# The next chunk's norm ahead of the gates in the plan of a state-space layer's second slot

## The chip, the cores and the metric

The kernel runs on one core of a Trainium2 chip. The metric is the device time of one execution in microseconds, the median over runs. The kernel before has 25287.4 us (3 runs, 25274.87 to 25290.24).

## The reference

Four layers on x of shape (8, 192, 56, 56) in float32, each `x = x + layer(group_norm(x))`: an involution (layer 0) and three selective state-space layers. The change touches layer 1, which is cut here to what matters:

```python
xn = layer_norm(tokens(group_norm(x)))           # over the 192 channels, L = 3136 tokens an image
xs = three slices of 64 channels, each a sequence of its own (3 * 8 sequences)
xi, z = split(xs @ in_proj_W.T)                  # 512 + 512
xc = silu(depthwise_conv4(xi));  dt, B, C = parts of xc @ x_proj_W.T, dt through softplus
h[t] = h[t-1] * exp(dt * A) + dt * xc * B[t]     # 512 x 16 states
y = (sum over states of h * C + xc * D) * silu(z)
out = proj(layer_norm(y @ out_proj_W.T + skip * xs))
```

## The kernel before, in words

The tokens of an image are cut into 7 chunks of T = 448, so there are 56 chunks. A chunk of layer 1 is three jobs, one for each slice of 64 channels; the code calls the slice a slot (0, 1, 2). A job is 16 units: 4 blocks `j` of 128 inner channels by 4 quarters `q` of the 16 states. A chunk has 48 units; the text numbers them 0 to 47, 16 to 31 being slot 1's.

A unit k does on each engine, in the order of the loop in `ssm_layer`:

- DVE: two scans (`scan`, L758), one for each half of its rows, and for even units the input product `inputs_by_vector` (L754) of unit k+1; in the last unit of a block (`q == 3`) the gate product `gated` (L792).
- POOL: for odd units the input product `inputs_by_pool` (L748) two units ahead, then `readout` (L767), the product with C, of unit k-2. So POOL's queue reads: inputs 35, readout 31, readout 32, inputs 37, and so on.
- ACT: the decays (`da`, L729) of the next unit, the start values (L737), and `keep` (L762), which stores the last state once both scans are done and which the readout waits for.
- PE: `reduce` of unit k-3 (L776, with L773 ahead of it at the first unit of a block, which waits for `gated`), the B row for `inputs_by_vector` (`spread_b`, L723) two units ahead, and filler matmuls (`nothing`, L782).
- SP issues the DMAs, in the order of the program: the loads of a block's operands (`load_ops`, `rep<-ops`, L713, four DMAs), which wait for their buffer; rows of B for POOL's inputs and of C for its readouts (`row_in`, `rows<-bc`, L629). B's rows for the next job's units 1 and 3 are issued in units 13 and 15 of a job, C's four rows in a job's first four units.

Beside the scan of one job the next job is prepared: convolution, projections, softplus, gates. These steps are spread over the 32 half units of a job by `places`, each step with a cost, over stretches that `bounds` sets. For slot 1's job, which prepares slot 2, the last stretch has half units 22 to 31, and it holds the gate steps of slot 2 and, in this job alone, the layer norm of the next chunk: `gates` (L1039) adds `norm()` (L972) of the next chunk where `i == 2`. The plan of a half unit is run (`bg.run`) ahead of the half unit's scan. A step's `rest`, such as an eviction, is called when a later step asks for it by its number `left`.

`norm()` is: normalize (L330, ACT, in place in `xg`), an average over channels (PE, L537), subtract (DVE, L543) and square (ACT, L545), the second average (L537), Ln and Exp (ACT, L549, L550), scale (DVE, L554), affine (ACT, L559), and `slices`: two small copies on ACT (L986, L987), or two memsets on POOL (L982, L983) for an image's first chunk, and eight DMAs from SP into `xs` (L991). `xs` has two buffers. The first convolution of the next chunk's slot 0 (L1026) reads it, and that one is prepared in slot 2's job, from its first half unit on. A gate step is one matmul (L1044) and its eviction to `zs` (ACT, L674). PE's short outputs share two PSUM banks (`mm_tile`).

The costs that `places` spreads are given with the steps, and a pause is a step that does nothing:

```python
return [
    Step(lambda: average(t), center, 0, nk), flushed(), pause(1.5),
    Step(lambda: average(lambda: st["sq"]), rstd, 0, nk), flushed(), pause(),
    Step(None, scale, 0), pause(1.5), Step(None, affine, 0), pause(),
]
```

Of the kernel before, what the change touches and what calls it, by code (L numbers as in the profile page):

```python
# [49 lines left out]
def pause(cost=1.0):  # L50
    return Step(None, lambda: None, 9, cost)
# [35 lines left out]
def conv_mamba_stack(ctx: ExitStack, tc: tile.TileContext, a, out):  # L87
# [16 lines left out]
    def mm_tile():  # L104
        return banks.mm.tile([128, 512], F32, tag="mm", name="mm")
# [424 lines left out]
    def layer_norm_steps(pool, t, p, nk, gam, bet):  # L530

        st = {}

        def average(src):
            st["ps"] = mm_tile()
            for i in range(nk):
                nc.tensor.matmul(  # L537
                    st["ps"][:p, :T], lhsT=lavg[:p, :p], rhs=src()[:, i, :], start=(i == 0), stop=(i == nk - 1)
                )

        def center():
            v, pm = t(), st["ps"]
            nc.vector.tensor_sub(v, v, pm[:p, :T].unsqueeze(1).to_broadcast([p, nk, T]))  # L543
            st["sq"] = pool.tile([CP, 3, T], F32, tag="sq", name="sq")[:p, :nk, :]
            nc.scalar.activation(st["sq"], v, AF.Square)  # L545

        def rstd():
            pv = st["ps"]
            nc.scalar.activation(pv[:p, :T], pv[:p, :T], AF.Ln, bias=eps[:p, :])  # L549
            nc.scalar.activation(pv[:p, :T], pv[:p, :T], AF.Exp, scale=-0.5)  # L550

        def scale():
            v, pv = t(), st["ps"]
            nc.vector.tensor_mul(v, v, pv[:p, :T].unsqueeze(1).to_broadcast([p, nk, T]))  # L554

        def affine():
            v = t()
            for i in range(nk):
                nc.scalar.activation(v[:, i, :], v[:, i, :], AF.Identity, bias=bet[:, i : i + 1], scale=gam[:, i : i + 1])  # L559
# [6 lines that stand above are left out]
# [105 lines left out]
    def evict(w, dst, src, m):  # L671

        if w.inb is None:
            nc.scalar.copy(dst, src)  # L674
        else:
            nc.scalar.activation(dst, src, AF.Identity, bias=w.inb[:, m : m + 1])  # L676

    def gate_steps(pool, w, u, z_mm, z_cost):

        zps = {}  # L680

        def gate(j):
            zps[j] = z_mm(j)

        def gate_out(j):
            if j == 0:
                u.zs = pool.tile([128, w.nd, T], F32, tag="zs", name="zs", bufs=2)
            evict(w, u.zs[:, j, :], zps[j][:, :T], w.nd + j)

        return [Step(lambda j=j: gate(j), lambda j=j: gate_out(j), 1, z_cost) for j in range(w.nd)] + [pause(0.5)]  # L690
# [274 lines left out]
    def mamba_jobs(pool, w):  # L965
        jobs = []
        chunks = Chunks(pool, 1)
        cks = chunks.all
        for ck in cks:
            c = ck.c  # L970

            def norm(c=c, ck=ck):  # L972
                def gnorm():
                    ck.xn = chunks.normalized(ck, None, 1)

                def slices():

                    xn = ck.xn
                    xs = pool.tile([128, 3, T + 3], F32, tag="xs", name="xs", bufs=2)
                    ck.xs = xs  # L980
                    if c == 0:
                        nc.gpsimd.memset(xs[:64, :, 0:2], 0.0)  # L982
                        nc.gpsimd.memset(xs[64:, :, 0:3], 0.0)  # L983
                    else:
                        before = cks[ck.place - 1].xs
                        nc.scalar.copy(xs[:64, :, 0:2], before[:64, :, T : T + 2])  # L986
                        nc.scalar.copy(xs[64:, :, 0:3], before[64:, :, T : T + 3])  # L987
                    for h in range(2):
                        for p0, p1, i, src in ((0, 64, 0, xn[0:64, 0, :]), (0, 32, 1, xn[64:96, 0, :]),
                                               (32, 64, 1, xn[0:32, 1, :]), (0, 64, 2, xn[32:96, 1, :])):  # L990
                            nc.sync.dma_start(out=xs[64 * h + p0 : 64 * h + p1, i, 2 + h : T + 2 + h], in_=src)  # L991

                return (
                    [Step(None, gnorm, 2)] + layer_norm_steps(pool, lambda: ck.xn, CP, NCT, g96, b96)
                    + [Step(None, slices, 2)]
                )

            ck.norm = norm

            def finish(c=c, ck=ck):  # L1000
                pps = {}

                def proj(t):
                    pps[t] = mm_tile()
                    for i in range(3):
                        nc.tensor.matmul(
                            pps[t][:CP, :T], lhsT=w.projw[:, i, t * CP : (t + 1) * CP], rhs=ck.y[:, i, :],
                            start=(i == 0), stop=(i == 2),
                        )

                def add(t):
                    nc.vector.scalar_tensor_tensor(
                        ck.x[:, t, :], pps[t][:CP, :T], w.projb[:, t : t + 1], ck.x[:, t, :], ALU.add, ALU.add
                    )

                return layer_norm_steps(pool, lambda: ck.y, 64, 3, g64, b64) + [
                    Step(lambda t=t: proj(t), lambda t=t: add(t), 1, 3) for t in range(NCT)
                ] + [pause()] + chunks.leave_steps(ck)

            for i in range(3):  # L1020

                def prepare(u, *beside, i=i, ck=ck, norm=norm):
                    def conv_mm(j):
                        pm = mm_tile()
                        for k in range(2):
                            nc.tensor.matmul(  # L1026
                                pm[:, :T], lhsT=w.inconv[:, k, j * 128 : (j + 1) * 128],
                                rhs=ck.xs[:, i, 2 - 2 * k : 2 - 2 * k + T], start=(k == 0), stop=(k == 1),
                            )
                        return pm  # L1030

                    convs, *others, stores = project_steps(pool, w, u, conv_mm, 2, *beside)
                    if i == 0:
                        stores = stores + [Step(None, lambda: chunks.fetch_next(ck), 2)]
                        if ck.place == 0:
                            convs = norm() + convs
                    return convs, *others, stores

                def gates(u, i=i, ck=ck):  # L1039
                    after_gates = cks[ck.place + 1].norm() if i == 2 and ck.place + 1 < len(cks) else []  # L1040

                    def z_mm(j):
                        pm = mm_tile()
                        nc.tensor.matmul(  # L1044
                            pm[:, :T], lhsT=w.inz[:, j * 128 : (j + 1) * 128], rhs=ck.xs[:64, i, 2 : T + 2], start=True, stop=True
                        )
                        return pm

                    return gate_steps(pool, w, u, z_mm, 1) + after_gates

                def after(u, i=i, ck=ck, finish=finish):
                    def out_proj():
                        u.ps = mm_tile()
                        nc.tensor.matmul(u.ps[:64, :T], lhsT=skip_d, rhs=ck.xs[:64, i, 2 : T + 2], start=True, stop=False)
                        for j in range(4):
                            nc.tensor.matmul(u.ps[:64, :T], lhsT=w.outw[:, j, :], rhs=u.zs[:, j, :], start=False, stop=(j == 3))

                    def leave():
                        if i == 0:
                            ck.y = pool.tile([64, 3, T], F32, tag="y", name="y")  # L1060
                        nc.scalar.copy(ck.y[:, i, :], u.ps[:64, :T])

                    def fetch():
                        if i == 2:
                            chunks.fetch_again(ck)

                    return fetch, [Step(out_proj, leave, 1, 5)], finish() if i == 2 else []

                jobs.append((i, c == 0, prepare, gates, after))
        return jobs  # L1070

# [74 lines left out]
    with ExitStack() as stack:  # L1146
        banks.y = stack.enter_context(tc.tile_pool(name="ps_iy", bufs=1, space=PSUM))
        banks.mm = stack.enter_context(tc.tile_pool(name="ps_im", bufs=6, space=PSUM))
        pool = stack.enter_context(tc.tile_pool(name="inv", bufs=1))
        with tc.manual_schedule():  # L1150
            involution(pool)
    for layer, w in enumerate((w1, w2, w3), 1):
        with ExitStack() as stack:
            scan_banks(stack)
            pool = stack.enter_context(tc.tile_pool(name=f"ssm{layer}", bufs=1))
# [75 lines left out]
```

## Time and profile before

| | |
|---|---|
| median of 3 runs | 25287.4 us |
| the profiled execution | 25314.83 us |
| its span | 25313.0 us |
| PE, mean granted clock | 83% busy, 0.827 |
| DVE | 89% busy, 22641.3 us |
| ACT | 67% busy, 16946.5 us |
| POOL | 92% busy, 23383.1 us |
| scans L758 (8064) | 15928.1 us, 2011 ns each |
| readouts L767 (4032) | 14746.3 us, 3675 ns each |
| inputs on POOL L748 (2016) | 8038.2 us, 3987 ns each |

Busy shares are means over the whole span, in which layer 1 is about 1630 to 17380 us. An idle time is put down to what ended it: `A <- B` means that A stood until B was done. In a timeline the columns are start and length in us, engine (SPq is SP's issue of DMAs), line, operation, output and inputs, a count of merged instructions, and in brackets the idle time ahead with what ended it. A DMA's length there is its issue, not its transfer.

### The profile page before, as it was taken

To read this page: it belongs to the slowest core of one execution; us is meant where nothing else is said; L and a number is where in the kernel's file an instruction comes from. 1 tells how busy PE (TensorE), PEld (TensorE's weight loads), DVE (VectorE), ACT (ScalarE), POOL (GpSimd) and SP (SyncE) were. 2 spreads that over 40 slices of the span, in tenths; PEclk is the share of its full clock that TensorE was granted. 3 is DMA by queue.
4 is the path that set the end of the run, shared out by engine and by line. 5 is a ranking of instruction groups with operands and counts; after the bars stand their busy time and mean duration, and the time that the engine had idled before them with its cause. 6 is when DMAs were issued, how large, how long until landed. Compare 5 with 4: busy or idle time off the path is not lost.

```text
span 25313.0 us, 232064 instructions
## 1 busy us (share of the span) xinstructions
PE 21123.4 (83%) x71870; PEld 6720.0 (27%) x71870; DVE 22641.3 (89%) x15661; ACT 16946.5 (67%) x32354; POOL 23383.1 (92%) x6772
## 2 busy tenths in 40 slices
PE   9988888888888888888888888888888887888888
PEld 3322222222222222222222222222333332333332
DVE  8879988998899889998998899897999998999998
ACT  1137776767766776766776676676777776777776
POOL 4469999999999999999999999998999998999999
PEclk9988777877777777777777787778888888888888
DMA  4433333333333333333333333333444443444443
GB/s 106 105 101 123 122 119 117 122 121 119 118 122 121 119 120 119 123 119 119 123 119 120 121 120 118 121 119 108 139 141 136 139 140 120 141 138 139 138 145 128
DMA packets 1184872, 3132.61 MB, mean 124 GB/s; under 512 B 163756, under 2 KB 446404, under 8 KB 1183496
## 3 DMA queue, kind: packets, MB, share of 16 engines
q1 hardware_dynamic: 1180824, 3116.70, 37.9%
q8 instruction: 564, 9.24, 0.1%
q14 instruction: 684, 5.60, 0.1%
q10 hardware_dynamic: 2800, 1.06, 0.0%
HBM read 2399.92 MB, written 555.55 MB: 117 GB/s over the span
## 4 chain that ended last, share of the span: by engine, by line
DVE 29%; PE 25%; ACT 19%; issue 11%; POOL 9%; DMA 6%; SPq 2%; DVEq 0%; POOLq 0%; ACTq 0%
DVE uhg L758 20%; ACT da L729 8%; DVE uhg L754 6%; POOL uhg L767 6%; PE y L776 4%; PE mm L635 4%; POOL uhg L748 3%; PE mm L416 3%; DMA rows<-bc 3%; PE y L782 2%; ACT L569 2%; PE y_inv L451 2%; PE y L773 2%; PE mm L612 2%; DMA rep<-ops 2%
## 5 line engine op out<-in xcount | busy, mean ns | idle before, releaser
L758 DVE TENSOR_TENSOR_SCAN uhg<-da,uhg 128x898 f32<-128x898 f32 x8064 | 15928.1, 2011 | 1284.0 <-ACT da L729 1261.9
L767 POOL TENSOR_TENSOR uhg<-uhg,rows 128x1792 f32<-128x1792 f32 x4032 | 14746.3, 3675 | 654.5 <-ACT carry L762 425.9
L729 ACT ACTIVATE da<-rep,k 128x448 f32<-128x448 f32 x16128 | 10255.9, 636 | 1816.6 <-DVE uhg L758 1438.7
L748 POOL TENSOR_TENSOR uhg<-rep,rows 128x1792 f32<-128x1792 f32 x2016 | 8038.2, 3987 | 375.5 <-DMA rep<-ops 206.2
L776 PE MATMUL y<-uhg,k 128*32 128x448 f32 x32256 | 4756.8, 666 | 562.0 <-POOL uhg L767 560.2
L754 DVE TENSOR_TENSOR uhg<-rep,b 128x1792 f32<-128x1792 f32 x2016 | 4031.8, 2000 | 658.9 <-PE b L723 615.1
L762 ACT COPY carry<-uhg 128x4 f32<-128x4 f32 x4032 | 787.3, 195 | 3514.0 <-DVE uhg L758 3464.3
L773 PE MATMUL y<-xc,w_d 128*128 128x448 f32 x2016 | 1522.0, 850 | 1580.5 <-DVE zs L792 1580.3
L782 PE MATMUL y<-w_d,k 128*128 128x448 f32 (+1 forms) x5166 | 2465.1, 586 | 0.0
L1026 PE MATMUL mm<-xs,k 128*128 128x448 f32 x2688 | 1289.7, 617 | 479.6 <-DMA xs<-xg 318.7
L776 PEld LDWEIGHTS y<-uhg,k 128*32 128x32 f32 x32256 | 695.1, 117 | 3664.1 <-issue 2204.0
L1082 PE MATMUL mm<-v,w_in 96*128 96x448 f32 x2688 | 1427.9, 662 | 199.7 <-ACT zs L676 92.4
L635 PE MATMUL mm<-dbl,w_dt 36*128 36x448 f32 (+1 forms) x2016 | 1469.0, 840 | 127.0 <-ACT k L617 127.0
L782 PEld LDWEIGHTS y<-w_d,k 128*128 128x128 f32 x5166 | 1035.4, 215 | 1486.5 <-issue 1459.8
L436 POOL TENSOR_TENSOR x<-x,one 96x448 f32<-96x448 f32 x560 | 633.3, 1135 | 668.3 <-DVE one L428 650.7
L612 PE MATMUL mm<-dbl,k 16*16 16x448 f32 x1120 | 692.7, 707 | 515.7 <-ACT dbl L605 515.7
L428 DVE TENSOR_TENSOR prod<-mm,shifted 128x448 f32<-128x448 f32 x1680 | 932.6, 609 | 207.8 <-PE mm L416 187.3
L1109 PE MATMUL mm<-xin,w_conv 128*128 128x448 f32 x2688 | 1076.4, 543 | 2.0 <-ACT xin L674 1.0
L773 PEld LDWEIGHTS y<-xc,w_d 128*128 128x128 f32 x2016 | 455.0, 265 | 2191.9 <-DVE zs L792 1509.5
L647 PE MATMUL mm<-xc,k 128*128 128x448 f32 x2016 | 983.7, 599 | 31.1 <-DVE dt L650 30.3
L723 PE MATMUL b<-k,k 96*128 96x448 bf16 x2016 | 819.1, 406 | 129.9 <-DVE uhg L754 129.8
L593 ACT ACTIVATE xc<-mm,k 128x448 f32<-128x448 f32 x1008 | 615.3, 627 | 438.9 <-PE mm L1026 327.1
(134 smaller groups left out, 19720.0 us busy)
## 6 DMA issues: line engine op xcount, KB each, us to landing
rep<-ops SPq DMA_DIRECT2D x4032, 448.0 KB, 5.7
ops<-dt SPq DMA_DIRECT2D x1008, 448.0 KB, 3.3
rows<-bc SPq DMA_DIRECT2D x1792, 224.0 KB, 6.2
shifted<-xpad SPq DMA_DIRECT2D x672, 179.0 KB, 4.6
xg<-stream SPq DMA_DIRECT2D x168, 336.0 KB, 3.7
xr<-stream SPq DMA_DIRECT2D x168, 336.0 KB, 5.3
stream<-xr SPq DMA_DIRECT2D x112, 336.0 KB, 3.2
xs<-xg SPq DMA_DIRECT2D x224, 112.0 KB, 6.1
```

Source lines behind the costliest of these rows:

```text
L612: nc.tensor.matmul(u.left[m][:NS, :T], lhsT=ident[:NS, :NS], rhs=u.dbl[:NS, :], start=True, stop=False)
L635: nc.tensor.matmul(u.dps[j][:, :T], lhsT=w.dtw[:, j * 128 : (j + 1) * 128], rhs=u.dbl[:nk, :], start=True, stop=True)
L729: nc.scalar.activation(t[:, 64 + 449 * r : 512 + 449 * r], reps[k // NQ][:, 2 * h + r, 0, :], AF.Exp, scale=w.neg_a[:, j * NR + 2 * h + r, ...
L748: nc.gpsimd.tensor_mul(uhg[k][:, :, 1:], reps[k // NQ][:, :, 1, :], b)
L754: nc.vector.tensor_mul(uhg[k][:, :, 1:], reps[k // NQ][:, :, 1, :], b)
L758: nc.vector.tensor_tensor_scan(v, banks.da[h][:, 63:961], v, 0.0, ALU.mult, ALU.add)
L767: nc.gpsimd.tensor_mul(v, v, us[i].rows[1, q].unsqueeze(1).to_broadcast([128, NR, T]))
L773: nc.tensor.matmul(ys[k // NQ][:, :T], lhsT=w.dd[:, j, :], rhs=us[i].xc[:, j, :], start=True, stop=False)
L776: nc.tensor.matmul(y[32 * r : 32 * r + 32, :T], lhsT=fold, rhs=uhg[k][:, r, 1:], start=False, stop=(q == NQ - 1))
L782: nc.tensor.matmul(ys[k // NQ][:, : nd * 112], lhsT=zeros, rhs=w.dd.rearrange("p j e -> p (j e)")[:, : nd * 112], start=False, stop=False,)
L1026: nc.tensor.matmul(pm[:, :T], lhsT=w.inconv[:, k, j * 128 : (j + 1) * 128], rhs=ck.xs[:, i, 2 - 2 * k : 2 - 2 * k + T], start=(k == 0), st ...
L1082: nc.tensor.matmul(pm[:, :T], lhsT=w.inw[:, k, m * 128 : (m + 1) * 128], rhs=ck.v[:, k, :], start=(k == 0), stop=(k == NCT - 1),)
```

## The change

In the list of steps that `gates` returns, the next chunk's norm comes first and the four gate steps after it. The list's costs, and the stretch over which they are spread, stay the same. It concerns the 55 jobs that scan slot 1 of a chunk with a chunk behind it.

```diff
                 def gates(u, i=i, ck=ck):
-                    after_gates = cks[ck.place + 1].norm() if i == 2 and ck.place + 1 < len(cks) else []
+                    normed = cks[ck.place + 1].norm() if i == 2 and ck.place + 1 < len(cks) else []
...
-                    return gate_steps(pool, w, u, z_mm, 1) + after_gates
+                    return normed + gate_steps(pool, w, u, z_mm, 1)
```

## The prediction

> **What bounds the kernel now.** I read the page first (busy times, costliest groups), then the waits of layer 1 alone, then the timeline of one chunk boundary engine by engine. The edit touches layer 1 only (1632 to 17380 us of the span), so one row of the busy times by stretch sets the scene; its columns are PE, PEld, DVE, ACT, POOL, granted clock, DMA share and GB/s:
>
> ```profile
> 1632.00:17380.00 15748.00, 12801.13 (x40062) 3735.45 (x40060) 14149.18 (x8559) 10986.03 (x20990) 15077.12 (x4046) 0.79 0.36 120
> ```
>
> POOL is busy 15077 of 15748 us. It is idle for 671 us in the whole layer, and no reordering that leaves POOL its work can win more. DVE has 1599 us idle. These are the longest waits there:
>
> ```profile
> DVE uhg L758 <- ACT da L729: 715.2, 415, 3.8
> DVE uhg L754 <- PE b L723: 572.0, 276, 5.8
> ...
> POOL uhg L767 <- ACT carry L762: 378.1, 365, 4.0
> POOL uhg L767 <- DMA rows<-bc: 224.6, 56, 5.1
> ...
> PE mm L1026 <- DMA xs<-xg: 318.7, 56, 8.1
> ```
>
> POOL waits 56 times, once a chunk, about 4 us, for a row of C (`rows<-bc`), and PE waits 56 times, once a chunk, 5.7 us, for `xs`. Both DMAs leave by SP. One boundary (slot 1 of chunk 25 ends, slot 2 begins), SP, then PE, DVE and POOL:
>
> ```profile
> 8839.82 1.31 SPq L629 DMA_DIRECT2D rows<-bc  x2
> 8861.25 2.97 SPq L713 DMA_DIRECT2D rep<-ops  x4
> 8864.37 7.96 SPq L991 DMA_DIRECT2D xs<-xg  x8
> 8872.44 2.52 SPq L629 DMA_DIRECT2D rows<-bc  x4
> ...
> 8872.95 3.32 PE L1026 MATMUL mm<-xs,k 128*128 128x448 f32 x4 [5.72 <-DMA xs<-xg]
> ...
> 8876.68 2.02 DVE L754 TENSOR_TENSOR uhg<-rep,b 128x1792 f32<-128x1792 f32 x1 [4.89 <-PE b L723]
> ...
> 8860.05 3.67 POOL L767 TENSOR_TENSOR uhg<-uhg,rows 128x1792 f32<-128x1792 f32 x1 [1.46 <-ACT carry L762]
> 8863.68 3.98 POOL L748 TENSOR_TENSOR uhg<-rep,rows 128x1792 f32<-128x1792 f32 x1
> 8867.63 3.65 POOL L767 TENSOR_TENSOR uhg<-uhg,rows 128x1792 f32<-128x1792 f32 x1
> 8875.61 3.67 POOL L767 TENSOR_TENSOR uhg<-uhg,rows 128x1792 f32<-128x1792 f32 x1 [4.33 <-DMA rows<-bc]
> ```
>
> The norm is the last thing in slot 1's plan, so its eight `xs` copies leave in the last unit, behind four `rep` loads. They take 7.96 us to issue: the last two stand until those loads land (releases at 8869.58 and 8871.81). Behind them on SP stand the four rows of slot 2; the first leaves at 8872.44, lands at 8875.48, and POOL idles 4.33 us. PE stands 5.72 us at slot 2's first convolution, the B row (L723) queued behind it is late, and DVE idles 4.89 us. Both of the busiest engines lose their time to one late step, so the loss is on the path. The copies start at 8584.45, 8864.37 and 9144.19 in three chunks running: 279.9 us a chunk.
>
> **The change, by parts.** Each of 55 chunks (the last has no next) moves one norm: on ACT normalize 2 x 0.70, square 0.95, Ln and Exp 0.58 + 0.52, affine 2 x 0.70; on PE two averages of 1.74 and 1.67; on DVE subtract 1.08 and scale 1.08; on SP eight copies; on ACT two small copies (0.19 + 0.20), which for an image's first chunk are two memsets on POOL (0.10 each). Four gate matmuls (3.51 together) and four evictions (about 0.5 each) go the other way. Nothing is removed; the filler matmuls of the stretch go from 5 to 6 (0.46 us, on PE, hidden while PE waits). In half units counted 22 to 31 from the plan's costs:
> before: gates 22, 22, 23, 23; normalize and average 24; subtract 26; second average 27; Ln, Exp 28; scale 29; affine and copies 31.
> after: normalize and average 22; subtract 23; second average 24; Ln, Exp 26; scale 27; affine 28; copies and two gates 29; gates 30 and 31.
>
> I place the moved steps on the shown chunk; unit numbers count 48 a chunk, so slot 1 is 16 to 31.
>
> *DVE.* PE ends the folds of unit 24 at 8839.76, where the gates start now; the average starts there instead and ends 8841.5. DVE is free at 8840.17, so subtract waits 1.43 us (it waits 1.31 now, two units later). The second scan of unit 27 starts at 8842.6 for 8840.08, and by unit 29 the moved 1.08 us and its wait are given back: 8848.4 for 8848.26. Scale follows in unit 29 at 8852.3 without its present wait of 0.68, as Ln and Exp now end a unit ahead of it. Unit 31 scans at 8859.7 for 8860.17: 0.45 us gained.
>
> *SP.* The affine starts on ACT when the decays of unit 30 end (8856.9), its first half ends near 8857.6, and the first copy leaves at 8857.7 for 8864.37. No rep load is ahead of it: the previous DMAs landed by 8846.7 (6.3 us after 8840.47). Copies that wait for nothing leave every 0.62 us (8866.21, 8866.85, 8867.49), so eight take 5.0, to 8862.7. The fifth, the last that slot 2's first convolution needs, leaves at 8860.2 and lands by 8866 at the median under load (6.1): the convolution, due about 8867, does not wait.
>
> *What the copies are moved past.* Here the change adds a wait. Now the second row of the pair at 8839.82, B's row for unit 35, leaves 24 us early. In the new order it stands behind the copies, and SP stands still for the affine: it leaves at 8862.7 for 8840.47. Behind it come the four rep loads (8863.4 to 8865.9, for 8861.25) and then C's row for unit 32 (8866.0, for 8872.44). How fast a row lands has two rows: 3.0 to 3.1 us behind `xs` copies (the three of 8872.44 to 8873.76), 6.3 right behind rep loads (8839.82). B's row is the first kind: 8865.7. C's row is the second: 8872.3.
> The Trainium skill, page "DMA: Bandwidth & Descriptors", section "Anatomy of one DMA — SWDGE (gpsimd) path", fits a transfer as about 2.0 us plus its bytes over 436 GB/s, for GpSimd's queue; an estimate from it for a 224 KB row is 2.5 us, below the 3.0 measured here for SP's, and with it POOL's chain below would gain another 0.5 us a chunk. The measured row is used.
>
> *POOL.* Readout 27 waits for the later scan (8844.9 for 8843.70); readout 30 starts at 8860.4 for 8860.05, so the 1.46 us gap moves forward and shrinks to a few tenths. POOL is free for inputs 35 at 8864.05, its row lands at 8865.7 and is seen at 8865.9: a new stall of 1.85. Then inputs (3.98) and readout 31 (3.65) put readout 32 at 8873.5 for 8875.61; its row landed at 8872.3. POOL gains 2.1 us there.
>
> *DVE at unit 33.* The convolution's bank is free when ACT has evicted the third gate, 8867.6; at half clock (3.32 for 4 records, as 8872.95 shows) it and the B row end near 8871.5, at full clock near 8870. DVE wants the row at 8871.3. So 4.89 of wait become 0 to 0.6, and with the 0.45 DVE gains 4.7 to 5.3.
>
> *Which of the two counts.* In layer 1 POOL holds DVE 7 times, 6.6 us in all (`DVE uhg L758 <- POOL uhg L767` among DVE's waits), while DVE's scans, through ACT's carry, hold POOL 365 times. So DVE runs ahead and POOL catches up in its own gaps. Averaged over chunks 7 to 54, the gaps ahead of readouts 42, 8, 12 and 14 of the units that follow are 0.85, 0.31, 0.75 and 1.19: 3.1 us that a later POOL fills, and another 1.57 at readouts 15 and 26. 2.1 + 3.1 = 5.2: POOL can follow. I take 4.9 us a chunk, 55 x 4.9 = 270 us. The profiled execution took 25314.8 us (span 25313.0 and 1.8 around it); 25314.8 - 270 = 25045. It is 27.4 above the median 25287.4, from which I subtract the same: 25017, said as 25020.
>
> **Rivals.**
> *PE's clock.* Rows of PE busy by stretch (columns as above):
>
> ```profile
> 8867.30:8870.70 3.40, 0.00 (x0) 0.00 (x0) 3.40 (x3) 2.39 (x7) 3.40 (x2) 1.00 0.99 280
> 8870.70:8877.60 6.90, 4.65 (x7) 2.33 (x8) 2.01 (x2) 1.87 (x4) 2.57 (x2) 0.51 0.53 178
> 8898.00:8901.50 3.50, 0.07 (x1) 0.08 (x2) 3.50 (x3) 2.92 (x7) 3.50 (x2) 0.99 0.00 0
> 8901.50:8921.90 20.40, 20.40 (x44) 4.94 (x45) 17.84 (x10) 14.45 (x30) 20.40 (x7) 0.50 0.28 94
> ```
>
> After an empty 3.4 us the clock halves. The second time it stays halved for 20.4 us though PE is busy throughout, and DVE waits for PE in unit 41 (1.4 us a chunk on average). PE's idle stretch before it is about 5.3 us, so a shift of 5 us against a window of 3.413 us (the spacing of the clock's records) can make it miss a whole empty window; then 1.4 more is won, and the chunk falls to near 80 windows, 273.1 (now 82: 279.9). Gain 6.3 to 6.8 a chunk, 347 to 374 us: 24913 to 24940. Against it: it can also halve elsewhere, and 81 windows (276.5, gain 3.4) is as near.
> The Trainium skill, page "TensorE: Matmul & The Clock Gate", section "Part 1: The HAM clock gate", says an idle window of about 3.4 us throttles PE and one busy window releases it, the window running free. The first half agrees with the rows above; the second does not (20.4 busy us at 0.50). By the rule PE would be at full clock from about 8905 and that wait would not be there to win.
> *POOL holds the gain.* If the catching up fails, only POOL's 2.1 us come, or 3.4 if the clock locks the chunk at 81 windows: 116 to 187 us, 25100 to 25172. For it: POOL's 96%. Against: who holds whom, above.
> *The wait only changes its place.* With the copies as slow as now (8.0) and B's row at the median of its line (6.2), it lands at 8871.9, 6.2 later than I put it. POOL's 2.1 become a loss of 4.1, of which its gaps take back 3.1 to 4.7: 55 lost to 33 won, 25254 to 25342, mostly no change that can be told.
> *Slower: SP held by the copies.* The same row decides. With copies at 8.0 and the row at the longest of its line (9.9), it lands at 8875.6: the stall is 9.9 longer than I put it, POOL at readout 32 is 7.8 behind today, its gaps give 4.7 back, and 3.1 x 55 = 170 us are lost: 25457. It decides from a landing past 8872.5. For it: a row that used to leave 24 us early now sits behind a wait for ACT. Against: the rep loads that slow the copies now come after them.
> That page on DMA says in the same section that any semaphore wait happens on the issuing sequencer ahead of dispatch, which is this rival's mechanism; the wait of SP from 8852.27 to 8861.21 agrees.
>
> **How the numbers follow.** Forecast (4 to 6 a chunk, 24960 to 25070) 0.47; clock 0.15; POOL holds 0.18; same place 0.10; slower 0.10. What a measurement of this kernel can tell from no change is about 0.2%, 50 us. Faster 0.80, same 0.10, slower 0.10. The range takes in the clock rival with a little more and POOL's rival with its 2.1: 24900 to 25210.
>
> **What would show it.** Right: the `xs` copies ahead of the rep loads on SP, about 5 us in all; `PE mm L1026 <- DMA xs<-xg` and `POOL uhg L767 <- DMA rows<-bc` gone; `DVE uhg L754 <- PE b` down by some 250 us; `POOL uhg L748 <- DMA rows<-bc` new, under 2 us each, 55 times; copies 275 us apart. Wrong: that new wait at 5 us or more, PE's half clock spreading in units 32 to 41, or chunks still 279.9 apart.

## The result, and the profile after

The changed kernel takes 25021.5 us (4 runs, 25018.75 to 25031.88) against 25281.1 (4 runs): ratio 0.9897, 95% interval 0.9885 to 0.9909. Its profiled execution took 25031.9 us, 282.9 below that of before; the forecast took 270 off.

The same boundary as before (slot 1 of chunk 25 into slot 2), in the timeline of the changed kernel: SP, then PE, DVE and POOL.

```profile
8724.55 4.98 SPq L991 DMA_DIRECT2D xs<-xg  x8
8729.57 0.59 SPq L629 DMA_DIRECT2D rows<-bc  x1
8730.28 2.49 SPq L713 DMA_DIRECT2D rep<-ops  x4
8732.86 8.05 SPq L629 DMA_DIRECT2D rows<-bc  x4
...
8734.49 1.77 PE L1026 MATMUL mm<-xs,k 128*128 128x448 f32 x4 [0.21 <-ACT zs L674]
...
8708.73 1.08 DVE L543 TENSOR_TENSOR xg<-xg,mm 96x896 f32<-96x896 f32 x1 [1.49 <-PE mm L537]
...
8738.17 1.98 DVE L754 TENSOR_TENSOR uhg<-rep,b 128x1792 f32<-128x1792 f32 x1
...
8732.75 3.99 POOL L748 TENSOR_TENSOR uhg<-rep,rows 128x1792 f32<-128x1792 f32 x1 [1.98 <-DMA rows<-bc]
8736.70 7.30 POOL L767 TENSOR_TENSOR uhg<-uhg,rows 128x1792 f32<-128x1792 f32 x2
```

The copies leave ahead of the rep loads and take 4.98 us for 7.96. The convolution waits 0.21 us, and not for `xs`; DVE's product of unit 33 (8738.17) has no wait ahead of it; POOL's readout 32 (the second of 8736.70) has none. In their place POOL waits 1.98 us for the B row, which now leaves behind the copies. The waits of layer 1 (to 17120 us), DVE's then POOL's; columns are total, times and longest:

```profile
DVE uhg L758 <- ACT da L729: 731.9, 407, 3.8
DVE uhg L754 <- PE b L723: 341.1, 221, 2.7
...
POOL uhg L767 <- ACT carry L762: 199.7, 171, 4.0
POOL uhg L748 <- DMA rows<-bc: 83.2, 42, 3.0
...
POOL uhg L748 <- PE y L782: 25.0, 13, 2.0
```

DVE's wait for the B row falls by 231 us (572.0 before), POOL's waits for DVE through the carry by 178, and POOL's wait for C's row (224.6) is gone. In its place stands the new one for B's row ahead of inputs 35, 2.0 us a chunk: the 83 us of its line, and the 25 that the view puts down to PE.

### The profile page after: what moved, and what is told of

It is laid out like the page before. It is cut to its first block, busy times and chain, and to the rows that moved or that the text cites. A ratio compares the mean times of both kernels' runs of the same rounds, so it can differ in the third digit from the quotient of the medians.

```text
span 25030.1 us, 232222 instructions
## 1 busy us (share of the span) xinstructions
PE 21294.5 (85%) x71980; PEld 6723.5 (27%) x71980; DVE 22624.9 (90%) x15661; ACT 16939.4 (68%) x32354; POOL 23378.2 (93%) x6772
## 4 chain that ended last, share of the span: by engine, by line
DVE 33%; PE 27%; ACT 17%; issue 11%; POOL 6%; DMA 5%; SPq 1%; DVEq 0%; POOLq 0%; ACTq 0%
DVE uhg L758 24%; ACT da L729 8%; DVE uhg L754 6%; PE y L776 4%; PE mm L635 4%; POOL uhg L767 4%; PE mm L416 3%; DMA rows<-bc 2%; PE y L782 2%; POOL uhg L748 2%; ACT L569 2%; PE y L773 2%; DMA rep<-ops 2%; PE y_inv L451 2%; PE mm L612 2%
## 5 line engine op out<-in xcount | busy, mean ns | idle before, releaser
L1026 PE MATMUL mm<-xs,k 128*128 128x448 f32 x2688 | 1211.5, 585 | 120.6 <-ACT zs L674 108.7
L1044 PE MATMUL mm<-xs,k 64*128 64x448 f32 x1344 | 860.6, 749 | 98.3 <-ACT zs L674 98.3
```

The source lines that it names most:

```text
L1026: nc.tensor.matmul(pm[:, :T], lhsT=w.inconv[:, k, j * 128 : (j + 1) * 128], rhs=ck.xs[:, i, 2 - 2 * k : 2 - 2 * k + T], start=(k == 0), st ...
```

## The experiments

Theory S is the prediction's: the order of the DMAs on SP, with DVE setting the chunk. G says that the gates' new place and PE matter, P that POOL's time counts us for us, D that DVE's alone does, C that PE's clock takes gains back. The table, to which the verdicts refer, has means over chunks 7 to 54 of each profile: us from one chunk's first scan to the next, DVE's idle time, and the parts of it at subtract and scale (units 27 to 30) and at the B rows of units 33 and 41, and POOL's idle time. The kernel before was measured again with each set of runs, at 25281 to 25309 us; a ratio is to the runs of its own set.

| kernel | median us | chunk | DVE idle | 27-30 | 33 | 41 | POOL idle |
|---|---|---|---|---|---|---|---|
| before | 25281 | 280.6 | 27.7 | 2.7 | 5.0 | 1.4 | 11.3 |
| changed | 25022 | 275.0 | 22.4 | 1.7 | 0.3 | 1.7 | 5.8 |
| e1 copies last | 25202 | 278.5 | 25.8 | 1.7 | 5.0 | 0.6 | 9.3 |
| e2 B row first | 25068 | 275.4 | 22.8 | 1.8 | 0.5 | 1.2 | 6.1 |
| e3 C row first | 25291 | 280.2 | 27.3 | 2.8 | 4.9 | 1.1 | 10.8 |
| e4 rows, copies, reps | 25035 | 275.3 | 22.3 | 3.0 | under 0.2 | 0.9 | 6.2 |
| e5 B row late | 25229 | 278.6 | 25.3 | 2.4 | 1.2 | 1.4 | 9.5 |
| e6 subtract later | 25075 | 276.1 | 23.7 | under 0.2 | 1.5 | 2.3 | 6.9 |
| e7 changed again | 25012 | 275.0 | 22.4 | 1.7 | 0.3 | 1.7 | 5.8 |
| e8 e6, rows first | 25076 | 276.2 | 23.7 | under 0.2 | 1.5 | 2.4 | 6.9 |
| e9 e6, fill 30 | 24826 | 272.0 | 19.0 | 0.3 | under 0.2 | 1.1 | 3.0 |
| e10 changed, fill 36 | 24974 | 274.1 | 21.4 | 1.9 | 0.6 | 0.5 | 4.9 |
| e11 e9, fill 36 | 24828 | 271.3 | 18.6 | 0.4 | under 0.2 | 0.9 | 2.3 |
| e12 changed, fill 30 | 25046 | 275.5 | 22.9 | 1.5 | under 0.2 | 2.1 | 6.3 |

**Is it the copies' place on SP?** e1 takes that alone out of the change:

```diff
-return normed + gate_steps(pool, w, u, z_mm, 1)
+return normed[:-1] + gate_steps(pool, w, u, z_mm, 1) + normed[-1:]
```

> The changed kernel, with the eight xs copies (and the two small ones on ACT) put back to the end of the plan, behind the gates; the norm's arithmetic and the gates stay where the change put them. Theory S (the order on SP): the copies stand again behind the rep loads, take about 8 us to issue, and both waits return (PE for xs about 5 us, POOL for the C row about 4 us a chunk): 25225 to 25300 us. Rival G (the gates and PE: the gain comes from gate matmuls that no longer jam PE in units 27 and 28 and that fill its idle time ahead of unit 31, so that its clock stays up): nothing is lost, 25010 to 25070 us.

25201.6 us, ratio 0.9969 (0.9958 to 0.9979), 23 us below S's range. Both waits are back in its layer 1:

```profile
DVE uhg L754 <- PE b L723: 546.2, 271, 6.2
...
POOL uhg L767 <- DMA rows<-bc: 190.6, 55, 5.1
```

S holds for the larger part, 180 of 260 us. The 80 that stay were not expected: the wait at scale is gone (27-30: 2.7 to 1.7) and that in unit 41 is 0.8 shorter.

e3 and e4 go the other way: the norm stays last, only SP's order is changed.

```diff
+if i + 1 < len(jobs) and jobs[i + 1][0] == 2 and m == per_job - 1:
+    us[i + 1].row_in(1, 0)
-if i and m < NQ:
+if i and m < NQ and not (m == 0 and jobs[i][0] == 2):
     us[i].row_in(1, m)
... (e4 has also, ahead of the first scan of a unit)
-load_when_free(k)
+if not (i + 1 < len(jobs) and jobs[i + 1][0] == 2 and m == per_job - 1):
+    load_when_free(k)
```

> The kernel before, norm last, with one DMA moved: the C row for unit 32 is issued in unit 31 ahead of the copies. POOL's wait for that row (4.1 us a chunk) should go. Theory S with DVE setting the chunk: DVE still waits 4.9 us for the B row behind the first convolution, and POOL then waits for DVE instead: 0 to 1 us a chunk, 25225 to 25285 us. Rival P: 4.1 x 55 = 227 us are won, about 25055 us. Rival G: nothing, 25281 us.

> The kernel before, norm last, with the C row of e3 ahead of the copies and the four rep loads of unit 31 put behind them: only the order on SP differs. The copies should take 5.0 us and the fifth leave near 8867 on the prediction's clock of chunk 25, so that the convolution starts 3 to 4 us earlier. Theory S: 3.6 to 4.9 us a chunk are won without moving the norm or a gate, 25010 to 25085 us. Rival G: no gate has moved, so nothing is won, 25281 us. Rival P: as e3, 25055 us.

e3: 25290.9, ratio 1.0001 (0.9992 to 1.0010). POOL's wait for the row (224.6 us) is gone and POOL waits almost as much longer for DVE, 203 us: its total for the carry was 378.1 in 365 waits.

```profile
POOL uhg L767 <- ACT carry L762: 580.7, 549, 4.0
```

So P falls: 4.1 us of POOL a chunk were worth nothing while DVE waited for PE.

e4: 25034.7, ratio 0.9902 (0.9888 to 0.9915), 251 us below its runs of before, within S's bounds with neither norm nor gate moved. G falls with it as the main cause. Its SP row has the copies in the time that the changed kernel gives them, though they leave as late as ever:

```profile
8742.49 4.98 SPq L994 DMA_DIRECT2D xs<-xg  x8
8747.52 2.53 SPq L713 DMA_DIRECT2D rep<-ops  x4
```

This order has a price of its own: POOL stands 3.3 us a chunk ahead of inputs 37, whose rep loads now leave behind the copies. It costs no time that can be told: the interval of e4 holds that of the changed kernel's ratio. The 80 us of e1 and the 251 of e4 are more than the change's 260, so the two gains overlap.

**What is POOL's new stall worth?** e2 takes it away, e5 makes it larger.

```diff
 e2, in unit 13 of slot 1's job, and no longer in unit 15:
+us[i + 1].row_in(0, 1)
+us[i + 1].row_in(0, 3)
 e5, in unit 15, behind load_when_free(k) instead of ahead of it:
+us[i + 1].row_in(0, 3)
```

> The changed kernel, with the B row for unit 35 issued together with the one for unit 33, ahead of the copies. The new stall of POOL ahead of inputs 35 (2.0 us a chunk in the changed kernel) should go under every theory. Theory S with DVE setting the chunk: POOL's time goes into its own gaps at readouts 14, 26 and 27, 0 to 0.5 us a chunk are won: 24995 to 25025 us. Rival P (POOL sets the chunk): 2.0 x 55 = 110 us are won, about 24910 us.

> The changed kernel, with the B row for unit 35 put one step further back on SP, behind the four rep loads as well as the copies: the cost that the slower rival named, made larger. The row should leave about 3 us later and land in about 6.5 us in place of 3, so that POOL's stall ahead of inputs 35 grows from 2.0 to 7 to 8.5 us. The prediction's account (POOL's own gaps take back what is left of them: about 0.7 + 0.3 + 1.1 + 1.3 = 3.4 us a chunk in the changed kernel): 5 to 6.5 less 3.4 is 1.6 to 3.1 us a chunk, 25110 to 25195 us. Rival P (every us of POOL counts): 5 to 6.5 x 55, 25295 to 25380 us. Rival D (DVE alone counts): 25021 us.

e2: 25068.4, ratio 0.9915 (0.9901 to 0.9928); e7, the changed kernel in the later set, 25011.8, 0.9893 (0.9880 to 0.9907).

> The changed kernel once more, for a comparison on the chip of e5, e6 and e8, and with e2 (25068 us), whose difference of 47 us is small: 25005 to 25050 us.

The stall goes and 0.8 of wait for the C row comes at readout 32; nothing is won, as S had it. That it should be some 50 us slower was not expected. The intervals of the ratios overlap, but each of its four runs (25038.8 and up) lies above each run of the changed kernel (25031.9 at most); it is left open.

e5: 25229.4, ratio 0.9979 (0.9970 to 0.9988). The stall grows from 2.0 to 7.8 us a chunk, as expected, but only 2.1 of the 5.8 come out of POOL's other gaps, not 3.4; the rest, 3.7, is 203 us in 55 chunks, and 208 to 218 are measured, above the range of the prediction's account. What POOL's other gaps take back costs nothing, and what they don't costs all: P and D are both wrong, and the prediction's slower rival is a real mechanism, met when the row comes about 6 us later.

**Where does DVE's next wait go?** The changed kernel's largest wait for PE between units 26 and 33 is at the subtract (1.7 us a chunk). e6 puts it a half unit later, e8 removes POOL's row waits as well.

```diff
+normed[2:2] = [pause(1.5)] if normed else []
 return normed + gate_steps(pool, w, u, z_mm, 1)
```

> The changed kernel with a pause of cost 1.5 behind the norm's first average, so that DVE's subtract stands one half unit later, and with it the second average; copies and gates stay in their half units. DVE's wait for PE at the subtract (1.68 us a chunk in the changed kernel) should be gone. If DVE's waits set the chunk: 1.4 to 1.7 x 55, 24930 to 24945 us. Rival C (the chunk is held near a whole number of PE's 3.413 us clock windows, so that a gain below a window mostly goes into other waits for PE): 24985 to 25060 us.

> e6 with both rows out of the way as well: the B row for unit 35 ahead of the copies (as e2), the C row for unit 32 between the copies and the rep loads. POOL's stalls at inputs 35 and readout 32 (2.0 in the changed kernel, 0.8 in e2) should be gone. If DVE sets the chunk, the rows bring nothing beyond e6: 24920 to 24950 us. If POOL counts beside it: another 1 to 2 us a chunk, 24830 to 24890 us. Rival C: 24985 to 25060 us.

e6: 25074.8, ratio 0.9921 (0.9909 to 0.9934), e8: 25076.5, 0.9920 (0.9907 to 0.9932), both above every range expected. The wait at the subtract is gone and the kernel is slower than the changed one: 1.2 us come back in unit 33, 0.8 in unit 17 and 0.7 in unit 41. Stretches around units 30 to 33 of one boundary (PE, PEld, DVE, ACT, POOL, granted clock, DMA share, GB/s), first of the changed kernel:

```profile
8720.80:8726.70 5.90, 1.52 (x3) 0.15 (x1) 5.90 (x5) 4.19 (x10) 5.90 (x2) 0.50 0.13 31
8726.70:8733.00 6.30, 6.25 (x16) 1.80 (x16) 6.30 (x4) 4.16 (x11) 4.32 (x3) 0.67 0.64 181
8733.00:8745.00 12.00, 10.18 (x44) 3.44 (x42) 12.00 (x7) 9.33 (x20) 12.00 (x4) 1.00 0.60 197
```

Then of e6, with the matmuls of its last three gates:

```profile
8744.00:8750.00 6.00, 0.29 (x1) 0.00 (x0) 6.00 (x4) 3.97 (x9) 6.00 (x2) 0.66 0.10 24
8750.00:8756.00 6.00, 5.71 (x13) 1.87 (x14) 6.00 (x5) 3.90 (x11) 4.38 (x2) 0.50 0.60 162
8756.00:8768.00 12.00, 12.00 (x35) 4.28 (x34) 10.21 (x7) 7.96 (x19) 11.71 (x4) 0.71 0.58 215
...
8753.73 4.85 PE L1044 MATMUL mm<-xs,k 64*128 64x448 f32 x6
```

In e6 nothing was left for PE to do for 6 us while DVE ran ahead to its gate product. Both kernels have a halved clock here. In the changed kernel it begins at 8720.6 and is over by 8730.8, ahead of the convolution (11.5 us on average). In e6 it begins at 8746.0, 1.7 us into the idle stretch, and lasts 17 us (15.5 on average; a chunk's halved time is 132.7 us for 122.7), so that the gates and the convolution, now on DVE's path, came late.

One thing beside it was taken apart by no run: 35 of the 48 chunks of e6 last a whole 81 windows of the clock (276.5 us, within 0.2), as 30 of the kernel before last 82, and in the changed kernel only one lasts a whole number. The lock to windows that the expectation of e6 named may so have a share in its loss.

e9 tests the idle place by giving PE something to do, e10 the same in another unit, e11 both, e12 the filling of e9 without e6's pause:

```diff
 e9, e12: in z_mm, ahead of the gate's own matmul
+for _ in range(8 if j == 0 and normed else 0):
+    nc.tensor.matmul(pm[:, :T], lhsT=zeros, rhs=w.dd.rearrange("p j e -> p (j e)")[:, :T], start=True, stop=True)
 e10: six of the same into u.left[0], ahead of left_of_b(0), for slot 0
```

> e6 (25075 us) with eight filler matmuls (128x448, about 0.46 us each, their result overwritten) ahead of the first gate of slot 2 in unit 30, where PE of e6 stands 6.0 us a chunk in one piece for DVE's gate product, after which its clock is halved for 15.5 us. Rival C (the gain of e6 was lost to PE's halved clock): the halved stretch from unit 30 goes, DVE's wait for the B row in unit 33 falls from 1.5 to 0.3 or less; that alone is 66 us, 25010 us, and with the other two waits that grew in e6 (units 17 and 41) 24940 us. If the clock is not the cause: the fillers change nothing or cost PE time, 25065 to 25110 us.

> The changed kernel (25012 to 25022 us) with six filler matmuls ahead of the first matmul on dbl of slot 0's preparation (in unit 36 to 37), where PE stands 4.3 us for ACT in 29 of 48 chunks, after which its clock is halved for 18 us in 30 of 48. Theory C: fewer or shorter halved stretches there, DVE's waits in units 40 and 41 (1.18 and 1.67) shrink by about 1.2: 24945 to 24975 us. If the clock is not what DVE waits for there: 25010 to 25050 us.

> e9 and e10 together: subtract a half unit later, and fillers in units 30 and 36. Theory C: the gains add, 24870 to 24960 us, which would be below both kernels. If the clock is not the cause: 25065 to 25130 us.

> The changed kernel (25012 to 25022 us) with the eight fillers of e9 in unit 30, the subtract where the change put it. It splits e9's gain. If the fillers only give back what moving the subtract had cost: DVE waits just 0.3 us for the B row in unit 33 of the changed kernel, so 0.3 to 0.8 us a chunk, 24970 to 25005 us, and the subtract is worth some 1.7 + 1.2 us a chunk once PE's clock holds. If the fillers alone make e9's time: 24820 to 24870 us.

e9: 24825.7, ratio 0.9811 (0.9798 to 0.9824), 249 us below e6, where 65 to 135 were expected. The same stretches, with the fillers and the same three gates:

```profile
8650.00:8656.00 6.00, 6.00 (x17) 2.67 (x15) 6.00 (x5) 4.37 (x11) 6.00 (x3) 1.00 0.13 33
8656.00:8662.00 6.00, 5.59 (x25) 1.58 (x24) 6.00 (x4) 3.90 (x10) 6.00 (x2) 1.00 0.63 189
8662.00:8674.00 12.00, 10.23 (x34) 3.92 (x34) 12.00 (x7) 9.34 (x20) 12.00 (x5) 0.86 0.56 197
...
8649.15 6.18 PE L1045 MATMUL mm<-w_d,k 128*128 128x448 f32 x16
8658.05 2.65 PE L1048 MATMUL mm<-xs,k 64*128 64x448 f32 x6
```

PE does more, its clock holds through the gates (2.65 us for 4.85), the convolution starts 1.8 us sooner behind unit 31's first scan (mean of chunks 7 to 53), and DVE is busy throughout and POOL too. That the eight fillers fill the whole idle place was luck: the expectation put them at 0.46 us each, 3.7 in all, and they take 6.18, with two records each.

e10: 24974.3, 0.9868 (0.9855 to 0.9882): 37 to 47 us below the changed kernel, at the upper end of the expected 24945 to 24975, and in the unit expected (41: 1.7 to 0.5). e11: 24827.7, 0.9812 (0.9799 to 0.9826), below the expected 24870 to 24960 but no better than e9: the gains do not add.

e12: 25046.4, 0.9900 (0.9884 to 0.9917), against an expected 24970 to 25005: without the later subtract the fillers gain nothing (unit 33's 0.3 goes, unit 41's wait grows by 0.4, unit 25's from 2.2 to 2.6). They do hold the clock there: its halved time in units 30 to 32 is 0.8 us a chunk for the changed kernel's 9.7. So a halved clock costs nothing that can be told where hardly any engine waits for PE. Neither edit pays alone, and the two together give 186 to 196 us: the pause removes a wait of DVE, and in unit 33 the fillers keep PE's clock from charging it again. For unit 33 C is shown; that is 1.5 of the 4.1 us a chunk between e6 and e9. The rest of the gain lies in other units (17, 25, 40, 41), where the halved stretches shift as no expectation said; how they do so stays open. e9 is the fastest of all with e11, 1.9% below before.

## Why the prediction came out right

*The path.* It named one late step holding both engines and DVE as the one that counts. e4 shows the first, with SP's order alone; e3 the second, where POOL's half was repaired and nothing was won.

*SP.* Copies in 5.0 us (4.98), B's row landing 3.0 us after its issue (8729.57 to 8732.59), C's 6.3 (8732.86 to 8739.64, 6.8), ahead of readout 32 at 8740.4: rows taken from the trace of before carried over to the new order.

*POOL.* Stall at inputs 35: 1.85 forecast, 2.0 measured. The gaps that a later POOL was to fill at readouts 42, 8, 12 and 14 (3.1 us) shrank to 0, 0, 0 and 0.7 with 0.15 or less counted as 0. As a general account, that POOL's gaps take back what they hold was too generous: for a further delay e5 shows 2.1 of the 3.4 that were left.

*DVE, by units.* Units 32 to 35 take 23.0 us for 27.7: 4.7, forecast 4.3 to 4.9 (and the wait left in unit 33 is 0.3, inside its 0 to 0.6). Units 24 to 31 take 49.0 for 50.4: 1.4 won where the sum had 0.45. That term was mis-sized, mainly because it was read from one boundary with a wait of 1.31 at the subtract; the mean of before is 1.8 there, with another 0.2 in unit 28. Units 24 and 25, for which the sum had no term, gave 0.2 more. (A filler matmul, put at 0.46 us, is two records and 0.92; it enters no term.) Against it the other units take 0.45 more, mainly at 41 and 17, for which the sum had no term.

*The total.* That makes 5.6 us a chunk from chunk 7 on for the 4.9 taken. Chunks 0 to 6 won 3.6 each (277.2 to 273.6), and layers 2 and 3, untouched, took about 8 us longer, so 282.9 us in the profiles and 260 in the medians stand about the forecast's 270 by errors that in part cancel.

*The rivals.* The clock did not give the extra gain: the halved stretch of 18 to 20 us from unit 37 or 38 on stays, and the wait in unit 41 grew. This rival rested in part on a misreading: PE's idle stretch there is 4.3 us in the trace of before (8897.15 to 8901.42), not 5.3. Nor is a whole empty window needed: at 8720.6 the changed kernel's clock halves behind a window of 3.41 us in which PE was busy for 1.7. POOL held nothing back within its slack. The chunks settled at no whole window: 273.4, 274.2, 275.3, 274.2, 275.3, 274.2 and 278.4 in an image. Their sum is 564 windows (1925.0 us); why it is whole stays open.

*Two rules of the Trainium skill.* The Trainium skill says in "DMA: Bandwidth & Descriptors", "Anatomy of one DMA — SWDGE (gpsimd) path", that a wait for a semaphore is done by the issuing sequencer ahead of dispatch. This trace agrees: B's row left 23 us ahead of its use in the kernel before (8840.47, for 8863.68), and in the changed one at 8729.57, just behind copies that SP held for ACT. In "TensorE: Matmul & The Clock Gate", "Part 1: The HAM clock gate", the Trainium skill has the clock halved after an idle window of about 3.4 us and released by one busy window. The first half agrees with the prediction's two rows and with e9, where work in the idle place kept the clock at 1.00, but it is too narrow: a window with 1.7 us of work was enough too (above). The second half does not agree: in e6 PE is busy from 8750.28 on and the full clock comes at 8763.04, 12.8 us later.

## What to carry to other kernels

A step that ends in DMAs costs its place in the issuing queue, not only its engine time: ask what stands in front of it, which transfers behind it were early only because nothing ahead of them waited, and when each of those is needed. Where two engines are both nearly full, repairing a wait of the one that follows was worth nothing while the other still waited (e3), and repairing both was worth nearly all of the gain (e4). Before a wait of the busiest engine is removed, look at what stands idle in that time: a PE that had little to do for a few us was slower afterwards, and cheap filler work was worth more than the wait (e6, e9), but only where an engine then waited for PE (e12).

## What the runs showed of the hardware

Eight matmuls without use, 6.2 us of PE's time a chunk, made a kernel 249 us faster (e6 to e9) whose PE was not its busiest engine. The granted clock behind the idle place went from 0.50 to 1.00; that this is the way of the gain is shown for the 1.5 us a chunk of unit 33 and not for the rest. Issue of eight copies from SP takes 4.98 us with nothing ahead of them and 7.96 behind four rep loads in flight: in the trace of before the seventh and eighth copy leave at 8869.60 and 8871.83, as loads issued eight DMAs earlier land (8869.58 and 8871.81), though they share no data with them. SP's DMAs there use eight completion semaphores in turn, and each issue waits for the one that it is to use again.
